# Interleaving the row blocks of a graph dilation, and pinning one load, in a two-layer graph network on one core

## The chip, the cores and the metric

The kernel runs on one core of a Trainium2 chip. A core has TensorE (PE, the matmuls; PEld is its weight loads), VectorE (DVE), ScalarE (ACT), GpSimd (POOL) and SyncE (SP), each with a queue of instructions that it takes in order. Sixteen DMA engines move data. Here SP issues the loads and POOL the stores. The metric is the device time of one execution in microseconds, as the median of several runs.

## The reference

There are 16 graphs (B) with 1024 nodes (N) and 128 features (D). `x` is B x N x D. `adj` is B x N x N with weights where there is an edge.

- **Layer 0**, three times per graph: `h @ W + b`, the cosine of all pairs of nodes, times `adj`, times `h`.
- **Dilation** of the graphs' patterns (`adj > 0`), which layer 1 needs. It is sequential in the rows: each row counts its neighbours, ranks them, removes those whose rank is a multiple of a step, and takes the same columns out of later rows:

```python
def step(carry, n):
    row = jnp.take(carry, n, axis=0)
    num = jnp.sum(row.astype(jnp.int32))
    sf = jnp.where(num > T_DIL, (num + K_DIL - 1) // K_DIL, 1)
    rank = jnp.cumsum(row.astype(jnp.int32))
    rm = row & (rank % sf == 0)          # and only where num > 1 and the mask is set
    carry = carry.at[n].set(row & ~rm)
    return carry.at[:, n].set(carry[:, n] & ~rm), None
```

- **Layer 1**, three graph convolutions ("sage" layers) on `adj * keep`, with a batch norm over all graphs behind each, then a projection and the residual `x2`, which is `x` after layer 0.

## The kernel before

**Two phases.** In the first, layer 0 and the dilation run side by side: layer 0 is mostly PE's work and dilation mostly DVE's and ACT's. In the second the three sage layers run, one after the other. In `residual` (L1055), within the last sage layer, each graph's `x2` is loaded back as `x2f` (L1058) and DVE adds it in (L1060, L1064). That tile has one buffer.

**Layer 0** (`layer0`, L439) is written as a generator that yields after each piece of work. Per graph and pass, `products` (L344) multiplies into a PSUM bank `pg`, of which there are two, and DVE multiplies the bank with `adj` into `ew` (L353 and L356), which empties it. `turn` (L373, L374) transposes `ew`, and `sums` (L384, L398) multiplies it with the features. Small tiles of PSUM share another two banks, `sm`: transposes, features, and dilation's `pdt`, `pT`, `pc` and `pe`.

**Dilation** (`dilation`, L545) goes through 16 blocks: 8 chunks `k` of 128 rows, each for two halves of 8 graphs. A block (`dilate`, L550) has three parts:

1. *Loads and tables* (L565 to L604). For each of 8 graphs, `an` (its rows of `adj`, L568) is loaded, and ACT makes the pattern of ones with Sign and Relu (L570, L571). For k > 0 what earlier chunks kept of these columns is loaded transposed as `kl` (L574), and DVE masks the pattern with it (L577). After every fourth graph, a table group: PE transposes the four diagonal blocks into `pdt` (L592), ACT copies them to `dT` (L594), PE makes `pT` (L599 to L601), and ACT writes the tables `T` (L603).
2. *Rounds* (L607 to L706). DVE finds zeros of T (`Z`, L615 or L618), then two to six rounds follow in which DVE compares (`E`, L650), PE counts (`pc`, L655 and L656), and DVE subtracts (L672). They end with a transpose of `E` (`pe`, L704, L705).
3. *Scans* (L709 to L744). For each graph DVE runs a cumulative sum over the 1024 columns (L722, `rank`, three buffers), ACT takes an absolute value (L731, Abs, one scan later in the text), DVE compares it into `kp` (L742), and POOL stores that as `keep` (L743).

The pattern has ten slots for eight graphs, so graphs 0 and 1 of the next block find a free slot, and graph i + 2 needs the slot that scan i of this block gives back. `an`, `kl`, `T` and `kp` have two buffers each.

**What sets the order.** `dilation` too yields a weight after each piece. The loop at L777 adds the weights up and runs layer 0's generator until it has come as far, in share of its own total, which it reaches at 0.93 of dilation's weight. This is the order of the program text. A planner then arranges each engine's queue: by its own estimates it may pull an instruction ahead of ones that stand before it in the text, if what it needs is there. `tc.keep_in_program_order` exempts an instruction from that; before, the Abs at L731 is the only one. In the hardware each queue is taken in order.

Of the kernel before, what the change touches and what calls it, by code (L numbers as in the profile page):

```python
# [16 lines left out]
P = 128  # L17
# [29 lines left out]
def tile_adj_preln_d2(  # L47
# [152 lines left out]
    with ExitStack() as actx:  # L200
# [344 lines left out]
        def dilation(exact=False):  # L545
            for k in range(NCH):
                for half in range(2):
                    yield from dilate(k, half, exact)

        def dilate(k, half, exact):  # L550
            nk = f"{'e' if exact else ''}{k}_{half}"
# [13 lines left out]
            for i in range(BH):  # L565
                b = half * BH + i
                an = poold.tile([P, N], F32, tag="an", name=f"an{nk}_{i}")
                nc.sync.dma_start(an, adj[b, cols, :])  # L568
                on = pattern(i)[:, 2 + k * P :]
                nc.scalar.activation(on, an[:, k * P :], AF.Sign)  # L570
                nc.scalar.activation(on, on, AF.Relu, accum_out=rest[:, i : i + 1])  # L571
                if k:
                    pk = poold.tile([P, NCH - 1, P], F16, tag="kl", name=f"kl{nk}_{i}")
                    nc.sync.dma_start(  # L574
                        pk[:, :k, :].rearrange("p j q -> p (j q)"), keep_d[b][: k * P, cols], transpose=True
                    )
                    nc.vector.scalar_tensor_tensor(  # L577
                        pattern(i)[:, 2 : 2 + k * P],
                        an[:, : k * P],
                        0.0,  # L580
                        pk[:, :k, :].rearrange("p j q -> p (j q)"),
                        ALU.is_gt,
                        ALU.mult,
                        accum_out=left[:, i : i + 1],
                    )
                yield 0.75
                if i % GT == GT - 1:
                    four = range(i - GT + 1, i + 1)
                    bs_ = slice(i - GT + 1, i + 1)
                    pdt = ps_sm.tile([P, GT, P], F16, tag="sm", name=f"pdt{nk}_{i}")  # L590
                    for n, ii in enumerate(four):
                        nc.tensor.transpose(pdt[:, n, :], pattern(ii)[:, diag], ident16)  # L592
                    dT = poold.tile([P, GT, P], F16, tag="dT", bufs=1, name=f"dT{nk}_{i}")
                    nc.scalar.activation(dT, pdt, AF.Copy)  # L594
                    nc.vector.tensor_scalar(rbias[:, bs_], rest[:, bs_], 2.0, -2.0, ALU.mult, ALU.add)
                    yield 0.1
                    pT = ps_sm.tile([P, GT, P], F32, tag="sm", name=f"pT{nk}_{i}")
                    for n, ii in enumerate(four):
                        nc.tensor.matmul(pT[:, n, :], lhsT=dT[:, n, :], rhs=upto, start=True, stop=False)  # L599
                        nc.tensor.matmul(pT[:, n, :], lhsT=pattern(ii)[:, diag], rhs=off, start=False, stop=False)  # L600
                        nc.tensor.matmul(pT[:, n, :], lhsT=ident16, rhs=after, start=False, stop=True)  # L601
                    for n, ii in enumerate(four):
                        nc.scalar.activation(T[:, ii, :], pT[:, n, :], AF.Identity, bias=rbias[:, ii : ii + 1])  # L603
                    yield 0.1  # L604


            x0 = poold.tile([P, BH], F32, tag="x0", name=f"x0{nk}")  # L607
            nc.vector.scalar_tensor_tensor(x0, left, -0.5, rest, ALU.add, ALU.add)
            nc.vector.tensor_tensor(x0, x0, mbias[:, half * BH : (half + 1) * BH, k], ALU.add)


            ends = exact or k >= LAST
            Z = poold.tile([P, BH, P], F16, tag="Z", name=f"Z{nk}")
            if ends:
                nc.vector.tensor_scalar(Z, T, 0.0, None, ALU.is_equal)  # L615
            else:
                found = poold.tile([P, 1], F32, tag="found", name=f"found{nk}")
                nc.vector.tensor_scalar(Z, T, 0.0, 0.0, ALU.is_equal, ALU.add, accum_out=found)  # L618
                nc.vector.tensor_tensor(astray[:, 0:1], astray[:, 0:1], found, ALU.add)
            E = poold.tile([P, BH, P], F16, tag="E", name=f"E{nk}")  # L620
            par = poold.tile([P, BH], F16, tag="par", name=f"par{nk}")

            def even(x, nm):

                ev = poold.tile([P, BH], F32, tag="ev", name=f"ev_{nm}")
                nc.vector.tensor_scalar(ev, x, EVENS, EVENS, ALU.add, ALU.subtract)
                return ev

            def removals(x, nm):


                if exact:
                    f, low = thresholds(x, nm)
                    at = poold.tile([P, 2, BH], F32, tag="at", name=f"at_{nm}")
                    nc.vector.scalar_tensor_tensor(at[:, 0, :], f, EVENS, low, ALU.subtract, ALU.max)
                    nc.vector.scalar_tensor_tensor(at[:, 0, :], x, 1.0, at[:, 0, :], ALU.is_le, ALU.add)
                    nc.vector.scalar_tensor_tensor(at[:, 1, :], f, EVENS, x, ALU.subtract, ALU.subtract)
                    nc.vector.tensor_tensor(par, at[:, 1, :], low, ALU.is_gt)
                    for i in range(BH):
                        nc.vector.tensor_scalar(  # L640
                            E[:, i, :], T[:, i, :], low[:, i : i + 1], at[:, 0, i : i + 1], ALU.max, ALU.is_equal
                        )
                else:
                    ev = even(x, nm)
                    mid = poold.tile([P, BH], F16, tag="mid", name=f"mid_{nm}")
                    nc.vector.scalar_tensor_tensor(mid, x, 1.0, ev, ALU.is_le, ALU.add)
                    if ends:
                        nc.vector.tensor_tensor(ev, ev, x, ALU.is_gt)
                        nc.vector.scalar_tensor_tensor(par, x, 1.0, ev, ALU.is_gt, ALU.mult)
                    nc.vector.tensor_tensor(E, T, mid.unsqueeze(2).to_broadcast([P, BH, P]), ALU.is_equal)  # L650
                pc = ps_sm.tile([P, BH], F32, tag="sm", name=f"pc_{nm}")
                for i in range(BH):
                    c = pc[:, i : i + 1]
                    if ends:
                        nc.tensor.matmul(c, lhsT=Z[:, i, :], rhs=par[:, i : i + 1], start=True, stop=False)  # L655
                    nc.tensor.matmul(c, lhsT=E[:, i, :], rhs=one16, start=not ends, stop=True)  # L656
                return pc

            if exact:
                x = poold.tile([P, BH], F32, tag="xe", bufs=1, name=f"xe_{nk}")  # L660
                nc.vector.tensor_copy(x, x0)
                with tc.For_i(0, P, 1):
                    pc = removals(x, f"e{nk}")
                    nc.vector.tensor_tensor(x, x0, pc, ALU.subtract)
            else:
                x = x0
                for r in range(ROUNDS[k]):
                    was = x
                    pc = removals(x, f"{nk}_{r}")
                    yield 1.0  # L670
                    x = poold.tile([P, BH], F32, tag="x", name=f"x_{nk}_{r}")
                    nc.vector.tensor_tensor(x, x0, pc, ALU.subtract)  # L672
                moved = poold.tile([P, BH], F32, tag="moved", name=f"moved_{nk}")
                nc.vector.tensor_tensor(moved, was, x, ALU.not_equal)
                nc.vector.tensor_tensor(astray, astray, moved, ALU.add)
            fin = poold.tile([P, 3, BH], F32, tag="fin", name=f"fin{nk}")
            radius, shift, none = fin[:, 0, :], fin[:, 1, :], fin[:, 2, :]
            if exact:

                f, low = thresholds(x, f"f{nk}")  # L680
                nc.vector.tensor_scalar(radius, x, 0.5, 0.5, ALU.add, ALU.mult)
                nc.vector.scalar_tensor_tensor(shift, f, EVENS, radius, ALU.subtract, ALU.subtract)
                nc.vector.tensor_tensor(radius, radius, low, ALU.max)
                nc.vector.scalar_tensor_tensor(shift, x, -2.0, shift, ALU.mult, ALU.add)
                nc.vector.scalar_tensor_tensor(radius, x, 1.0, radius, ALU.is_le, ALU.add)
            else:

# [473 lines left out]
```

## Time and profile before

| | us |
|---|---|
| median of 3 runs | 2893.7 (2886.03 to 2895.54) |
| the profiled execution | 2886.45 |
| its span, first to last instruction | 2884.7 |
| PE busy in it | 2661.2 (92%) |
| DVE busy | 1937.6 (67%) |
| ACT busy | 1427.3 (49%) |
| POOL busy | 468.7 (16%) |

PE's granted clock was 0.982 over the span. The first scan begins at 78 us and the last at 1563; layer 0's last matmul ends at about 1700, and the sage layers follow. A busy share that is an average over the span says little here, since the phases differ; so stretches and waits are read below.

In the profile, "A <- B" behind a wait means that A stood idle until B had released it. A row of a group has the line, engine, operation, output and inputs, shape and count, then the busy time in us with the mean of one in ns, then the idle time of the engine just before them with what ended it.

### The profile page before, as it was taken

What the parts mean: (1) busy time and instruction counts of PE and PEld (TensorE: products, weight loads), DVE (VectorE), ACT (ScalarE), POOL (GpSimd) and SP (SyncE); (2) the same over time, 40 slices, a digit from 0 to 9 for tenths busy, and PEclk for the clock granted to TensorE, in tenths of its full rate; (3) what the DMA queues carried; (4) which work ended last, traced back from release to release, by engine and by line L of the source; (5) the groups of instructions that cost most, each with busy time, mean ns of one, the idle gap of its engine ahead of it and who ended that gap; (6) DMA issues with size and microseconds to landing.
All of it is one profiled execution on the core that took longest, in us unless ns stands there. A gap on an engine that the chain in (4) does not pass through costs nothing. (4 is left out here: it accounts for less than half of the span.)

```text
span 2884.7 us, 52007 instructions
## 1 busy us (share of the span) xinstructions
PE 2661.2 (92%) x18803; PEld 2196.4 (76%) x18803; DVE 1937.6 (67%) x4913; ACT 1427.3 (49%) x4100; POOL 468.7 (16%) x619
## 2 busy tenths in 40 slices
PE   6899999899999999988998989999989999899997
PEld 4666676666666666666676779889879999899996
DVE  3788778877878788778877457777762333355554
ACT  6767667557556556455455333333333333333334
POOL 3111112011111111111112012222220010010101
PEclk9999999999999999999999999999999999999999
DMA  9447257347355475297063249999985666576764
GB/s 280 143 144 217 87 171 240 88 139 214 102 177 169 106 223 168 72 251 192 28 206 108 92 151 374 400 391 399 401 341 185 202 213 202 177 235 225 241 225 135
DMA packets 382234, 585.23 MB, mean 203 GB/s; under 512 B 85200, under 2 KB 266448, under 8 KB 381968
## 3 DMA queue, kind: packets, MB, share of 16 engines
q1 hardware_dynamic: 343280, 425.28, 47.1%
q0 software_dynamic: 38688, 156.53, 14.8%
q8 instruction: 151, 2.47, 0.4%
q14 instruction: 115, 0.94, 0.1%
HBM read 403.44 MB, written 163.58 MB: 197 GB/s over the span
## 5 line engine op out<-in xcount | busy, mean ns | idle before, releaser
L868 PE MATMUL agg<-hw,aT 128*128 128x128 f32 (+1 forms) x6144 | 742.9, 277 | 8.2 <-DVE aT L965 7.2
L868 PEld LDWEIGHTS agg<-hw,aT 128*128 128x128 f32 x6144 | 712.6, 192 | 13.3 <-DVE aT L965 9.7
L344 PE MATMUL pg<-nhT 128*128 128x512 f32 (+3 forms) x1152 | 457.2, 500 | 70.7 <-DVE ew L356 60.2
L384 PE MATMUL po<-ew,hS 128*128 128x512 f32 (+3 forms) x1152 | 457.4, 501 | 6.4 <-ACT hTo L407 3.6
L356 DVE TENSOR_TENSOR ew<-pg,adjA 128x768 f32<-128x768 f32 (+3 forms) x528 | 423.3, 824 | 0.5 <-PE pg L344 0.3
L398 PE MATMUL po<-ew,hS 128*128 128x128 f32 x2688 | 366.3, 276 | 0.0
L398 PEld LDWEIGHTS po<-ew,hS 128*128 128x128 f32 x2688 | 338.2, 192 | 35.4 <-issue 34.2
L374 ACT ACTIVATE ew<-gt 128x512 f32<-128x512 f32 (+1 forms) x480 | 209.0, 465 | 267.9 <-PE gt L373 260.6
L344 PEld LDWEIGHTS pg<-nhT 128*128 128x128 f32 x1152 | 189.3, 193 | 175.2 <-issue 130.4
L722 DVE TENSOR_TENSOR_SCAN rank<-patt 128x1024 f16<-128x1024 f16 x128 | 292.9, 2294 | 0.8
L384 PEld LDWEIGHTS po<-ew,hS 128*128 128x128 f32 x1152 | 196.4, 195 | 98.0 <-issue 67.3
L373 PEld LDWEIGHTS gt<-ident,ew 128*128 128x128 f32 x1344 | 169.8, 144 | 100.1 <-issue 74.8
L353 DVE TENSOR_TENSOR ew<-pg,adjA 128x128 f32<-128x128 f32 x384 | 107.2, 279 | 188.0 <-PE pg L344 142.8
L373 PE MATMUL gt<-ident,ew 128*128 128x128 f32 x1344 | 213.1, 278 | 4.3 <-PEq L802 2.4
L918 POOL TENSOR_TENSOR o<-o,rn 128x512 f32<-128x512 f32 x96 | 108.3, 1128 | 650.6 <-DVE rn L917 631.3
L840 PE MATMUL pw<-wrx,hT 128*128 128x256 f32 x768 | 180.5, 389 | 10.5 <-ACT hT L1032 9.7
L842 DVE TENSOR_TENSOR own<-pw,bs 128x256 f32<-128x256 f32 x192 | 81.3, 423 | 141.4 <-ACT hw L841 141.3
L840 PEld LDWEIGHTS pw<-wrx,hT 128*128 128x128 f32 x768 | 145.7, 195 | 32.9 <-ACT hT L1032 10.5
L913 ACT ACTIVATE own<-o 128x128 f32<-128x128 f32 x384 | 114.6, 301 | 111.1 <-DVE o L897 111.1
L897 DVE SCALAR_TENSOR_TENSOR o<-agg,invdeg,own 128x128 f32<-128x128 f32 x384 | 109.7, 344 | 86.9 <-PE agg L868 78.3
L983 ACT ACTIVATE aT<-pta 128x512 f32<-128x512 f32 (+3 forms) x160 | 71.2, 466 | 188.5 <-PE pta L982 180.7
L321 POOL TENSOR_TENSOR hS<-hN,rn 128x1024 f32<-128x1024 f32 x48 | 95.0, 1979 | 401.2 <-DVE rn L157 302.0
(165 smaller groups left out, 3940.4 us busy)
## 6 DMA issues: line engine op xcount, KB each, us to landing
an<-in_adj_dram SPq DMA_DIRECT2D x128, 512.0 KB, 4.7
keep<-kp POOLq DMA_DIRECT2D x128, 256.0 KB, 4.1
kb<-keep SPq DMA_DIRECT2D x128, 256.0 KB, 5.5
aT<-adT SPq DMA_DIRECT2D x32, 960.0 KB, 5.7
aT<-adT SPq DMA_DIRECT2D x32, 832.0 KB, 5.2
aT<-adT SPq DMA_DIRECT2D x32, 704.0 KB, 4.3
aT<-adT SPq DMA_DIRECT2D x32, 576.0 KB, 3.4
xb<-in_x_dram SPq DMA_DIRECT2D x31, 512.0 KB, 5.1
```

Of the source, the lines that this page charges most:

```text
L344: nc.tensor.matmul(pg[:, :n, :].rearrange("p c q -> p (c q)"), lhsT=self.nhT[:, q * P : (q + 1) * P], rhs=self.nhT[:, (q + c) * P : (q + c ...
L356: nc.vector.tensor_tensor(both[0][:, :, off, :], pg[:, own:n, :].unsqueeze(1).to_broadcast([P, 2, n - own, P]), both[1][:, :, off, :], ALU ...
L373: nc.tensor.transpose(pt[:, i, :], ew[:, at + i, :], ident)
L374: nc.scalar.activation(ew[:, at : at + n, :], pt[:, :n, :], AF.Copy)
L384: nc.tensor.matmul(self.po[:, c * P : (c + n) * P], lhsT=self.hS[:, q, :], rhs=ew[:, c - q : c - q + n, :].rearrange("p c q -> p (c q)"), ...
L398: nc.tensor.matmul(self.po[:, q * P : (q + 1) * P], lhsT=self.hS[:, q + n, :], rhs=ew[:, NCH - 1 - q + n, :], start=False, stop=closes and ...
L722: nc.vector.tensor_tensor_scan(rank, pt[:, 1 : N + 1], pt[:, 2:], 0.0, ALU.add, ALU.add)
L840: nc.tensor.matmul(pw[:, i, :], lhsT=hT[:, 2 * h + i, :], rhs=wrx[:, l, :], start=True, stop=True)
L868: nc.tensor.matmul(self.place(c), lhsT=aT[:, blk, :], rhs=self.hw[:, source, :], start=source == 0 and c % self.ga == 0, stop=ends(c, source),
L897: nc.vector.scalar_tensor_tensor(self.o[:, c, :], self.place(c)[:, :P], invdeg[:, b, c : c + 1], self.own[:, c, :], ALU.mult, ALU.add,)
L913: nc.scalar.activation(self.own[:, n, :], self.o[:, n, :], AF.Square, accum_out=ss[:, c : c + 1])
L918: nc.gpsimd.tensor_tensor(self.o[:, hc, :], self.o[:, hc, :], rn.unsqueeze(2).to_broadcast([P, CPH, D]), ALU.mult)
```

## The change

`dilate` no longer yields its work itself. It returns three generators, `loads`, `rounds` and `scans`, with the same instructions as before. `dilation` runs a block's rounds and then its scans, and after each of the eight scans takes one step of the next block's loads: one graph's pattern, and after the fourth and the eighth graph a table group. The first block's loads run ahead of its rounds as before, and the last block's scans have none beside them. A step of the loads yields 0.8 in place of 0.75 for each graph and 0.1 twice for each group. The exact variant, which runs only if a check on the data finds something (`n_off > 0`), keeps its order.

In `residual` the `x2f` load is exempt from the planner.

Cut to its core (the bodies of the three generators are the text above, indented):

```diff
         def dilation(exact=False):
-            for k in range(NCH):
-                for half in range(2):
-                    yield from dilate(k, half, exact)
+            blocks = [(k, half) for k in range(NCH) for half in range(2)]
+            loads = ()
+            for n, block in enumerate(blocks):
+                if not loads:
+                    loads, rounds, scans = dilate(*block, exact)
+                yield from loads
+                yield from rounds
+                this, loads = scans, ()
+                if n + 1 < len(blocks) and not exact:
+                    loads, rounds, scans = dilate(*blocks[n + 1], exact)
+                for scanned, weight in this:
+                    yield weight
+                    if scanned and loads:
+                        yield next(loads)
...
-            for i in range(BH):
+            E = radius = shift = low = None
+
+            def loads():
+                for i in range(BH):
...
-                yield 0.75
-                if i % GT == GT - 1:
...
-                    yield 0.1
...
-                    yield 0.1
+                    yield 0.8
+
+            def rounds():
+                nonlocal E, radius, shift, low
...
+            def scans():
...
-                    yield 2.5
+                        yield True, 2.5
...
-                yield 0.8
+                    yield False, 0.8
+
+            return loads(), rounds(), scans()
...
         def residual(b):
             x2 = pool2.tile([P, NCH, D], F32, tag="x2", bufs=1, name=f"x2f_{b}")
-            nc.sync.dma_start(x2, x2_d[b].rearrange("(c p) d -> p c d", p=P))
+            tc.keep_in_program_order(nc.sync.dma_start(x2, x2_d[b].rearrange("(c p) d -> p c d", p=P)))
```

## The prediction, made before the changed kernel ran

> **What bounds the kernel now.** I read the busy time of each engine in stretches first, then PE's waits, then the dilation's rows, then one piece of the timeline. The first answer cuts the run at 1580 us, where the last scan ends, and around 1700, where layer 0 ends. Its columns are the stretch, its length, and each engine's busy time with its number of instructions.
>
> ```profile
> 60.00:1580.00 1520.00, 1394.25 (x8745) 1012.80 (x8744) 1206.71 (x2842) 914.42 (x2431) 245.90 (x318) 0.98 0.53 156
> 1580.00:1700.00 120.00, 117.02 (x661) 84.65 (x660) 53.86 (x134) 37.64 (x114) 8.75 (x6) 1.00 0.19 65
> 1700.00:1740.00 40.00, 30.95 (x240) 28.97 (x238) 25.10 (x77) 15.36 (x44) 7.35 (x13) 0.91 0.88 316
> ```
>
> PE (first busy column) is what bounds it: busy for 1394 of 1520 us while dilation and layer 0 run together, and its work isn't touched. All that this part can give back is PE's idle time, 125.7 us. PE's waits there, longest first (total, times, longest):
>
> ```profile
> PE pg L344 <- DVE ew L356: 60.1, 41, 5.2
> PE pc L656 <- DVE E L650: 10.9, 13, 1.5
> PE pg L344 <- DVE rn L157: 7.2, 4, 2.8
> ```
>
> Half of it is one wait: layer 0's product needs one of two `pg` banks, and VectorE (DVE) hasn't emptied them. No later row is over 5.3 us. So I ask when DVE is late. The next two answers take blocks 2 to 15 (of 16): first the stretches from a block's first scan to its last `kp`, then what lies between them, where the next block's tables and rounds are made. These are the sums over the 14 stretches of each.
>
> ```profile
> sum 855.00, PE 761.54 PEld 546.60 DVE 738.86 ACT 547.60 POOL 160.52; mean PE 54.40 PEld 39.04 DVE 52.78 ACT 39.11 POOL 11.47
> ...
> sum 499.00, PE 480.73 PEld 357.46 DVE 344.53 ACT 251.15 POOL 60.86; mean PE 34.34 PEld 25.53 DVE 24.61 ACT 17.94 POOL 4.35
> ```
>
> Among scans DVE is 86.4% busy (738.86/855) and PE idles 93.5 us, 10.9%. Between them DVE is 69.0% busy and PE idles 18.3 us, 3.7%. That unevenness is what the change can level. The rows of the dilation itself:
>
> ```profile
> L722 DVE TENSOR_TENSOR_SCAN rank<-patt 128x1024 f16<-128x1024 f16 x128 | 292.9, 2294 | 0.8
> L731 ACT ACTIVATE rank<-rank,fin 128x1024 f16<-128x1024 f16 x128 | 145.9, 1146 | 0.4 <-DVE rank L722 0.4
> L742 DVE TENSOR_SCALAR kp<-rank,fin 128x1024 f16<-128x1024 f16 x128 | 74.3, 581 | 55.3 <-ACT rank L731 52.9 <-DMA keep<-kp 1.7
> L570 ACT ACTIVATE patt<-an 128x896 f16<-128x896 f32 (+7 forms) x121 | 79.5, 662 | 128.0 <-DMA an<-in_adj_dram 68.0 <-DVE rank L722 59.4 <-DVE kp L742 0.6
> ```
>
> **The change, part by part.** *Nothing is added or removed.* The same 128 scans, 112 masks (L577), 32 table groups and 128 `kp` are issued, with the same DMAs: per block 8 `an`, 8 `kl` (but for k = 0) and 8 `keep`. The weights that pace layer 0 agree too (8 x 0.8 = 8 x 0.75 + 4 x 0.1), so dilation ends beside the same layer-0 work; in the two instruction orders PE has equal layer-0 columns behind the last `pe`, within 1%. The tail of 120 us stays.
>
> *What moves.* I compared the orders of the built programs. The loads hardly move: in both, 91 of 112 masks stand between the scans of the block before, since the planner had already pulled each load up to the scan that frees its slot. SP's queue has the same runs of `an` and `kl`, and POOL's queue the same `keep` stores. So I price DMA and both queues at nothing; their cover is that the transfers had been early already. What moves is the spacing of scans and the tables. Counted in layer 0's `ew` instructions, a clock that PE sets, blocks 2 to 14 have 319 of 681 between their first and last scan before, and 389 after. With the rows' durations DVE then has 1.90 us of work for each `ew` among scans and 1.56 elsewhere before; 1.72 and 1.72 after. The level is even.
>
> *What evening is worth.* The two stretches give two points, idle 3.7% at 69% and 10.9% at 86.4%. On a straight line evening gains nothing: at the common 80% (1083.4/1354) PE idles the same 112 us. On a curve that grows as load/(1 - load), which fits both points (2.23 x 1.7 = 3.7; 6.35 x 1.7 = 10.8), 80% gives 6.8%, 92 us: a gain of 20 us, 21 with the first blocks. Ends: 0 and -21. Against the upper end, the small scale gets worse: neighbouring scans with at most one `ew` between them go from 20 to 30 of 127. I take two thirds, **-14**. This is my choice, not a row.
>
> *A rule against it.* The Trainium skill ("Perfetto Trace Analysis", Optimizing Scalar/DVE Operations) says that where Scalar or Vector isn't saturated but makes bubbles on another engine, breaking up instructions may help. A scan stays one piece of 2.29 us. By that rule alone the evening is worth 0; by the stretches -14. The wait row has 41 waits of 1.5 us on average and a longest of 5.2, over two scans long, so queues of several instructions matter besides the single scan; I keep the row's reading.
>
> *Tables among the scans: a wait added.* A table group on ACT is `dT` (0.59 us) and four `T` (0.37 each), 2.06 us, and waits for PE's `pdt` and `pT`, 25.1 + 25.0 us over 31 groups, 1.6 each. Before, no scan's Abs (L731) stands close behind a group; after, 15 of 32 groups have one directly behind, 26 within two layer-0 instructions. The skill ("PSUM — Partial Sum Buffer", Engine vs sequencer instructions) calls these queues strict FIFO; the `kp` row agrees, as its 52.9 us are waits for an Abs. Behind a late Abs stands `kp` on DVE, and behind that `ew`, whom PE waits for. At most 26 x 3.7 = 96 us of DVE stall. Below, it may be 0 or a gain, since `kp` now also stands further back and the Abs has more time. By the nearest row, 37 waits of 1.4 us, 26 more are 37 us of DVE time, in an engine that is idle a fifth of the time. I put a tenth on PE, 3.7: **+4**, with ends -10 and +48 (half of the 96).
>
> *x2's load.* The planner had pulled the last layer's first `x2f` load to the start of phase two:
>
> ```profile
> 1713.88 0.37 SPq L1058 DMA_DIRECT2D x2f<-x  x1
> ...
> 1725.20 0.87 DVE L1060 SCALAR_TENSOR_TENSOR x2f<-blb,mf,x2f 128x128 f32<-128x128 f32 x3 [7.87 <-DMA x2f<-x]
> ...
> 1727.81 0.50 PEld L982 LDWEIGHTS pta<-ident,aT 128*128 128x128 f32 x3 [6.83 <-issue]
> 1727.84 0.88 PE L982 MATMUL pta<-ident,aT 128*128 128x128 f32 x3 [6.69 <-issue]
> ```
>
> It lands after 11 us, DVE waits 7.87 us for it with the masks of row 4 behind, and PE stands still for 6.69 us. Pinned, the load goes to the last layer and the stall goes. Next late is the mask chain (L959, L965, L969, 1.6 us), whose rows were issued at 1708, so I take **-6**, ends -6.7 and 0. In that layer every `x2f` load now stands behind its batch's third `aT` row rather than ahead of the batch's first; behind it on SP wait five rows, and on DVE L897. PE is 60.00 of 60 us busy there, with a sums bank to spare, and a load of 5 us: 0, at worst +10.
>
> **Sum.** -14 + 4 - 6 = -16. Against the profiled execution's own time, 2886.45 (span 2884.7), that is 2870.5; the median of the runs shown, 2893.7, is 7.25 above that execution, and so I predict 2877.7, rounded to **2878 us**. A measurement of this kernel can tell about 0.3%, 8.7 us, from no change.
>
> **Rivals.**
> (a) *It doesn't do what it says:* the loads were early already, and the straight line holds. Only x2 remains: -6, 2888. For it: 91 of 112 both times, and more scan pairs. Against: 1.72 and 1.72.
> (b) *Slower:* ACT's queue takes the place of the evened load. At the Abs behind the table groups, 96 us of stall, half of which reaches PE: +48; with -14 and -6, and in place of the +4, it is +28, 2922. It makes the kernel slower than before once `kp`'s waits for the Abs, 52.9 us, grow by 40 (half of 40 uses up the 20). For it: 26 groups against none. Against: the planner set `kp` back as well, and T's 16 us of waits at `Z` (L615, L618) may shrink.
> (c) *Better than the curve:* the waits for `ew` halve (-30), and `kp` and `kl` waits fall with them (-10), and x2's -6: 2848.
>
> **How the numbers follow.** Forecast 47% (own range 2862 to 2890), (a) 20%, (b) 27%, (c) 6%. The range for 8 in 10 goes from 2850, close to (c), to 2910, which takes in the lower half of (b). Faster by over 0.3% (below 2885) are most of the forecast, a little of (a), and (c): 0.51. Within it are the rest of the forecast, most of (a) and the edge of (b): 0.22. Slower is (b) with a piece of (a): 0.27.
>
> **What will show it.** Right: PE's wait `pg` for `ew` falls from 60 to 45 us or less, the idle shares among and between the scans come close to each other, and the 6.69 us gap at `pta` is gone. Wrong: `kp`'s waits for the Abs grow beyond 80 us with PE's `pg` wait above 60 (b), or both shares stay put though the scans are spread (a). A PE gap in the last layer would make the zero for x2's new place wrong.

## The result, and the profile after

| | before | after |
|---|---|---|
| median of 20 runs, us | 2888.55 (2881.39 to 2895.54) | 2877.09 (2871.27 to 2890.45) |
| the profiled execution | 2886.45 | 2874.98 |
| its span | 2884.7 | 2873.2 |

The ratio is 0.9965, with a 95% interval of 0.9955 to 0.9975. So the kernel is faster by 0.35% (10 us) by the ratio, and by 11.5 us by the medians. The median of before, 2893.7 from three runs, came down to 2888.55 with twenty.

Where the 11.5 us came from is read by cutting both traces at the same events (us; in brackets the time in it in which PE stood idle; worked out from the instructions of the two traces; layer 0 is taken to end with its last multiplication with the features, `po`):

| stretch | before | after |
|---|---|---|
| start to first scan | 78.1 (25.6) | 77.0 (24.2) |
| first to last scan | 1487.6 (123.2) | 1478.4 (117.1) |
| to layer 0's last `po` matmul | 134.0 (3.0) | 133.7 (2.9) |
| to the second sage layer's first matmul of aggregation (`agg`, the 2049th) | 468.8 (41.0) | 469.3 (39.4) |
| the rest | 716.2 (30.8) | 714.8 (30.4) |

Nearly all of it is between the first scan and the last: 9.2 us, 6.1 of which are idle time of PE. The other 3.1 are a shorter busy time of PE, which isn't traced further. The lines of after stand 17 to 20 further down: the scan is L740, Abs L749, `kp` L760, `E` L667. The same stretches as before:

```profile
60.00:1570.00 1510.00, 1389.78 (x8737) 1013.20 (x8736) 1205.15 (x2858) 911.44 (x2428) 249.05 (x319) 0.98 0.53 157
1570.00:1689.00 119.00, 116.11 (x654) 84.36 (x653) 53.77 (x134) 37.10 (x113) 8.44 (x6) 1.00 0.19 66
1689.00:1729.00 40.00, 37.33 (x323) 35.01 (x321) 31.23 (x84) 18.22 (x53) 8.01 (x15) 1.00 0.89 321
1729.00:1769.00 40.00, 33.22 (x275) 31.79 (x275) 24.94 (x59) 12.20 (x41) 10.19 (x15) 0.91 1.03 376
```

The tail kept its length (119 us from last scan to cut, 120 before). In the first 40 us of phase two PE is 37.33 us busy where it was 30.95: the gap at `x2f` is gone. In the next 40 it is 33.22. The DMA share stands at 1.03 there (the last but one column). The timeline of after shows what happened:

```profile
1737.63 0.69 DVE L989 SCALAR_TENSOR_TENSOR aT<-aT,both 128x512 f32<-128x512 f32 x1 [6.51 <-DMA aT<-in_adj_dram]
...
1738.43 1.09 PE L1002 MATMUL pta<-ident,aT 128*128 128x128 f32 x4 [5.98 <-DVE aT L989]
```

The same `pta` waits 5.98 us again, 11 us later and for a row of the second graph: the wait moved. The DMA engines are full in this stage (1.03), which fits; the runs of part 1 show that it moves, not that this is why.

PE's waits up to layer 0's end (total, times, longest):

```profile
PE pg L344 <- DVE ew L356: 65.5, 52, 3.8
...
PE pc L673 <- DVE E L667: 4.0, 9, 0.8
...
PE pg L344 <- DVE rn L157: 1.0, 1, 1.0
```

The wait that the forecast was about, `pg` for `ew`, did **not** fall: 65.5 us after 60.1. The small one in the rounds, `pc` for `E`, fell from 10.9 to 4.0, and a small one of layer 0, `pg` for `rn`, from 7.2 to 1.0. Then the sums over the 14 stretches from a block's first scan to its last `kp`, and over the 14 between them:

```profile
sum 1098.00, PE 999.40 PEld 724.41 DVE 867.29 ACT 685.01 POOL 189.70; mean PE 71.39 PEld 51.74 DVE 61.95 ACT 48.93 POOL 13.55
...
sum 230.00, PE 222.66 PEld 167.25 DVE 201.42 ACT 103.09 POOL 30.85; mean PE 15.90 PEld 11.95 DVE 14.39 ACT 7.36 POOL 2.20
```

Among scans PE idles 98.6 us of 1098, 9.0%, with DVE 79.0% busy. Between them, where only rounds are left, it idles 7.3 of 230, **3.2%**, with DVE 87.6% busy. The more loaded stretch is the one that costs less. So one rising curve over DVE's load can't be right. The dilation's rows:

```profile
L740 DVE TENSOR_TENSOR_SCAN rank<-patt 128x1024 f16<-128x1024 f16 x128 | 295.0, 2316 | 0.9
L749 ACT ACTIVATE rank<-rank,fin 128x1024 f16<-128x1024 f16 x128 | 146.7, 1151 | 30.8 <-DVE rank L740 30.2 <-DVE fin L712 0.5
L760 DVE TENSOR_SCALAR kp<-rank,fin 128x1024 f16<-128x1024 f16 x128 | 68.6, 547 | 49.9 <-ACT rank L749 49.4
```

The counts are the same and the busy times nearly so, and `kp` waits for the Abs 49.4 us, where it waited 52.9: rival (b) isn't seen.

### The profile page after: what moved, and what is told of

Its sections match the earlier page's. It is cut to its first block, busy times and chain, and to the rows that moved or that the text cites. A ratio compares the mean times of both kernels' runs of the same rounds, so it can differ in the third digit from the quotient of the medians.

```text
span 2873.2 us, 51953 instructions
## 1 busy us (share of the span) xinstructions
PE 2659.3 (93%) x18803; PEld 2199.0 (77%) x18803; DVE 1939.7 (68%) x4913; ACT 1426.0 (50%) x4100; POOL 473.7 (16%) x619
## 5 line engine op out<-in xcount | busy, mean ns | idle before, releaser
L344 PE MATMUL pg<-nhT 128*128 128x512 f32 (+3 forms) x1152 | 460.2, 502 | 69.5 <-DVE ew L356 65.5
L740 DVE TENSOR_TENSOR_SCAN rank<-patt 128x1024 f16<-128x1024 f16 x128 | 295.0, 2316 | 0.9
L860 PE MATMUL pw<-wrx,hT 128*128 128x256 f32 x768 | 179.5, 388 | 10.5 <-ACT hT L1052 9.7
L860 PEld LDWEIGHTS pw<-wrx,hT 128*128 128x128 f32 x768 | 145.0, 194 | 32.6 <-ACT hT L1052 10.5
L749 ACT ACTIVATE rank<-rank,fin 128x1024 f16<-128x1024 f16 x128 | 146.7, 1151 | 30.8 <-DVE rank L740 30.2
```

The lines of the kernel that those rows point to most:

```text
L344: nc.tensor.matmul(pg[:, :n, :].rearrange("p c q -> p (c q)"), lhsT=self.nhT[:, q * P : (q + 1) * P], rhs=self.nhT[:, (q + c) * P : (q + c ...
L740: nc.vector.tensor_tensor_scan(rank, pt[:, 1 : N + 1], pt[:, 2:], 0.0, ALU.add, ALU.add)
L749: nc.scalar.activation(rank, rank, AF.Abs, bias=shift[:, i : i + 1], scale=1.0 if exact else -1.0)
L860: nc.tensor.matmul(pw[:, i, :], lhsT=hT[:, 2 * h + i, :], rhs=wrx[:, l, :], start=True, stop=True)
```

## The experiments

Each ratio is to the kernel before, timed on the same chip. The medians come from three chips, on which before took 2887.13 us (parts 1 and 2, and after with pinned scans), 2883.39 (before with pinned scans, and part 4) and 2888.35 (parts 5 to 7), so kernels of different parts are compared by their ratios. The letters in the expectations: in part 1, A says that the pin of `x2f` is worth nothing, and B that it is worth 6 us. From part 2 on, A says that the mean density of DVE's work sets what PE loses; C, that an Abs behind a table group costs; D, that the gain comes from tables being ready early; E, that PE's `pg` waits are made by scans that the planner puts close together; G, that the length of one scan makes them.

**1. The pin by itself, both ways.** The first kernel is after without it, the second is before with it.

```diff
-            tc.keep_in_program_order(nc.sync.dma_start(x2, x2_d[b].rearrange("(c p) d -> p c d", p=P)))
+            nc.sync.dma_start(x2, x2_d[b].rearrange("(c p) d -> p c d", p=P))
```

> The changed kernel with x2's load not exempt from the planner, so that the first x2f load stands at the start of phase two again. Theory A (all of the gain is dilation's; phase two is bound by its DMA there, so the 6.7 us gap that went at row 4 of the first graph came back as a 6.0 us gap in the second): as the changed kernel, 2877 within 4 us, and the stretch from the first to the 2048th agg matmul stays at 459 to 460 us. Theory B (the pin is worth the 6 us that were forecast): 2883.

> The kernel before, with the pin alone. Theory A (the pin is worth nothing): 2888 within 4 us, a ratio of 0.999 to 1.001. Theory B (it is worth 6 us): 2882, a ratio of 0.998. Either way dilation's part of the span, up to layer 0's last matmul at 1700 us, is as before within 3 us.

Without it 2880.06 us, 0.9979 of before (0.9964 to 0.9993). With it alone 2888.08, 0.9997 (0.9986 to 1.0009), so the forecast 6 us (0.2%) lie outside the interval, which leaves at most 4. Without it the median is 3 us above after's, and the two intervals overlap, so that run alone decides nothing. The timeline of before with the pin has a gap at the same place as after:

```profile
1745.52 0.83 PE L982 MATMUL pta<-ident,aT 128*128 128x128 f32 x4 [4.87 <-DVE aT L969]
```

After without the pin has the gap where before has it (6.42 us, at 1717.5 us) and none over 2 us at the second graph. From the first `agg` to the second sage layer's first it takes 458.1 us with the pin alone, 459.3 before, 459.8 after and 459.1 in after without it. The pin is worth nothing that shows here.

**2. The masks among the scans, the tables behind them.** After, but each table group (PE's `pdt` and `pT`, ACT's `dT` and `T`) waits until the block's last scan, as in before:

```diff
+                    yield 0.75
+                for i in range(BH):
                     if i % GT == GT - 1:
...
-                    yield 0.8
+                        yield 0.2
```

> The changed kernel, but only the patterns of the next block are made among the scans; both of its table groups (pdt, dT, pT, T) stand behind the last scan, as before the change. Theory A (the gain is the lower density of VectorE work among scans, and a table group has hardly any VectorE work): within 4 us of 2877. Theory C (an Abs behind a table group in ScalarE's queue costs some us, which the changed kernel pays): faster than it, 2870. Theory D (the gain is that tables are ready sooner, so that rounds start without a gap): back to 2886.

2898.75 us, 1.0044 of before (1.0029 to 1.006): slower than both. Its waits, of PE and then of DVE:

```profile
PE pg L344 <- DVE ew L356: 59.6, 46, 3.3
PE pc L675 <- DVE E L669: 11.2, 13, 2.2
```

```profile
DVE Z L637 <- ACT T L620: 24.3, 8, 4.8
```

The same wait of `Z` in before, then in after:

```profile
DVE Z L618 <- ACT T L603: 11.7, 5, 4.2
```

```profile
DVE Z L635 <- ACT T L618: 14.8, 7, 3.7
```

`pc` waits 11.2 us again, as before: where the tables are made moves this wait, some 7 us. D's own reason isn't seen. `Z` waits for the tables longer after the change than before (14.8 against 11.7), and in all three traces it starts only 0.1 to 0.2 us behind the last table on average. What goes with `pc` is how much of layer 0 stands beside the rounds: between `Z` and the first scan of blocks 2 to 16 DVE has 106 `ew` in before, 155 in after and 107 here.

`pc` is the smaller part of what this order loses. It is 0.8% (23 us) slower than after, more than A, C or D expected. Between first and last scan PE idles 139.9 us, where it idles 117.1 in after, and `pg` isn't higher. The rest is spread over small waits of layer 0, such as `pt_a` for its load (11.1 after 7.3), `pt_h` for `x` (9.2 after 6.2) and `po` for `hTo` (8.2 after 5.4). Why they grow stays open.

**3. The spacing of scans by itself.** In after, 30 of 127 neighbouring scans have at most one `ew` between them on DVE, in before 20. The text doesn't put them so: the planner pulls scans forward. Exempt from the planner, each scan stays where the text has it:

```diff
-                        nc.vector.tensor_tensor_scan(rank, pt[:, 1 : N + 1], pt[:, 2:], 0.0, ALU.add, ALU.add)
+                        tc.keep_in_program_order(
+                            nc.vector.tensor_tensor_scan(rank, pt[:, 1 : N + 1], pt[:, 2:], 0.0, ALU.add, ALU.add)
+                        )
```

The same edit was made in after and in before:

> The changed kernel with every scan exempt from the planner, so that it stays where the text puts it: neighbouring scans with at most one ew between them fall from 30 of 127 to 10, while VectorE's work and its mean density among the scans stay. Theory A (mean density alone sets TensorE's idle time): 2877 within 4 us and a wait of pg for ew of 60 to 65 us. Theory E (runs of scans set it): the wait falls below 50 us, and the time to 2865.

> The kernel before, with every scan exempt from the planner (and nothing else): neighbouring scans with at most one ew between them fall from 20 of 127 to 3. Theory E (what TensorE loses among scans is set by runs of scans on VectorE): the wait of pg for ew falls from 60 us to below 40, and the time by 30 us or more, to 2857 or less. Theory A (mean density sets it): the density among scans stays, 2888 within 5 us. If E holds, its distance to the changed kernel with pinned scans (2827) is what the interleaving is worth when scans do not run in pairs: under 10 us if spacing was all, some 30 us if the level of the density counts as well.

In after it gives 2826.9 us, 0.979 of before (0.9773 to 0.9806): 50 us faster than after, far more than expected. In before it gives 2844.42, 0.9863 (0.9839 to 0.9886). PE's waits, first of after so pinned, then of before so pinned:

```profile
PE pg L344 <- DVE ew L356: 37.5, 36, 3.2
...
PE pc L673 <- DVE E L667: 3.6, 8, 0.8
```

```profile
PE pg L344 <- DVE ew L356: 40.1, 42, 3.7
...
PE pc L656 <- DVE E L650: 10.6, 13, 1.5
```

This tells two effects apart. `pg` falls to some 40 us in both, interleaved or not, once the close pairs of scans are gone (10 and 3). `pc` falls only where the tables are made early. That is E for the large wait, and the place of the tables for the small one. With pinned scans, too, the interleaved kernel is faster, by 0.7% (21 us; 0.9863 against 0.979; the intervals don't meet), but see 5 for the scatter. That lies between the "under 10" of spacing alone and the "some 30" of a level that counts as well. In the traces PE idles 13.0 us less for it between first and last scan (94.6 and 81.6), more than the 7 of `pc`.

**4. Which instruction makes the wait?** Three variants of after with pinned scans: masks pinned as well (as the scan above, at L594); masks and `kp` pinned; the Abs freed:

```diff
-                    tc.keep_in_program_order(
-                        nc.scalar.activation(
-                            rank, rank, AF.Abs, bias=shift[:, i : i + 1], scale=1.0 if exact else -1.0
-                        )
+                    nc.scalar.activation(
+                        rank, rank, AF.Abs, bias=shift[:, i : i + 1], scale=1.0 if exact else -1.0
```

> The changed kernel with scans pinned and the masks of the next block (L594) pinned too: masks that stand directly beside a scan fall from 33 of 112 to 7, stretches of over 6 us of VectorE work between two ew from 38 to 32. Theory E: some 5 to 10 us below 2827, with the wait of pg for ew below 37 us. Theory A: 2827 within 4 us. Risk: a pinned mask waits for its load at its place, and VectorE's waits for kl grow.

> As the one with scans and masks pinned, and kp pinned as well: one pair of neighbouring scans, 27 stretches of over 6 us of VectorE work between two ew. Theory E: a little faster again, 2815 to 2822. Against it: with three kinds of instruction fixed, waits of VectorE for Abs and loads at fixed places (55 us for Abs with scans pinned) grow, and the time rises above 2830.

> The changed kernel with scans pinned, but the Abs no longer: the planner then moves it ahead of the table groups on ScalarE, so that an Abs stands within two instructions behind a group 1 time in place of 25. It also sets scans closer against ew: 27 neighbours in place of 10. Theory C (the Abs behind a table group costs): VectorE's waits of kp for Abs fall from 55 us to under 30. If that wait is what TensorE pays for, the time falls below 2820; if pairs of scans weigh more (theory E), it rises to 2850 or so although the waits of kp fall.

| pinned | us | ratio to before | close scans | `pg` for `ew` | `kp` for Abs |
|---|---|---|---|---|---|
| Abs (before) | 2888.55 | 1 | 20 | 60.1 | 52.9 |
| Abs (after) | 2877.09 | 0.9965 (0.9955 to 0.9975) | 30 | 65.5 | 49.4 |
| Abs, scans | 2826.9 | 0.979 (0.9773 to 0.9806) | 10 | 37.5 | 55.5 |
| Abs, scans, masks | 2845.21 | 0.9869 (0.9846 to 0.9891) | 7 | 26.5 | 60.3 |
| Abs, scans, masks, `kp` | 2835.04 | 0.9832 (0.9812 to 0.9852) | 1 | 18.4 | 58.0 |
| scans | 2857.13 | 0.9908 (0.9884 to 0.9933) | 27 | 58.6 | 14.6 |

Read the last three columns together. The kernels with 20 close scans or more have 58.6 to 65.5 us of `pg`, those with 10 or fewer 18.4 to 37.5 (before with pinned scans, above: 3 and 40.1). It is two groups rather than a slope: the late tables of part 2 have 31 close scans and 59.6 us, so going from 20 to 30 isn't shown to cost anything. The runs vary what is pinned; that the closeness of scans makes the wait, and not something else in the new orders, is read from these counts. `kp`'s wait for the Abs doesn't go with it at all. With the Abs free it falls to 14.6 us, and yet `pg` is back at 58.6, with 27 close scans again, as E expected. The expectations for pinned masks, alone and with `kp`, missed: `pg` fell, but the time rose, with masks alone by 0.8% (0.9869 against 0.979). PE idles 96.9 us there between first and last scan, where it idles 81.6 with pinned scans only. Other waits had grown, such as the one for features, 11.4 us in that kernel after 4.1, and in the kernel with all pinned:

```profile
PE pg L344 <- DVE ew L356: 18.4, 27, 3.2
...
PE po L384 <- ACT hTo L407: 13.3, 13, 2.1
```

**5. Is it luck of the planner's order?** Two kernels with weights shifted a little (`yield 0.8` to 1.0 for a load, 2.5 to 2.3 for a scan), the first on after, the second on after with pinned scans:

```diff
-                    yield 0.8
+                    yield 1.0
...
-                        yield True, 2.5
+                        yield True, 2.3
```

> The changed kernel with the weights of a load and a scan at 1.0 and 2.3 in place of 0.8 and 2.5, the same sum: nothing is pinned, added or moved to another part of the text, only the spacing shifts a little and the planner's choices with it. This measures how far an equal kernel scatters. If the 10 us of the change are the interleaving's: within 5 us of 2877. If they are within the planner's luck: more than 8 us off, to either side.

> The same weights with scans pinned. As above: within 5 us of 2827 if an order of this kind has a time of its own, 8 us or more off if the scatter of equal orders is as large as the steps between the kernels with pinned scans (2827, 2835, 2845).

On after: 2876.46 us, 0.9955 (0.9939 to 0.997), with `pg` at 60.7 and `pc` at 3.0. So the change's 10 us hold under another order. On pinned scans: 2838.15, 0.9818 (0.9793 to 0.9842). By the medians that is 11 us above the kernel it was made from, by the ratios 8 (the intervals overlap), and in the two traces layer 0 ends 8.4 us later. So two equivalent orders with pinned scans can lie some 10 us apart. In part 4 the kernel with all pinned lies 12 us above the one with scans and Abs pinned, by the ratios, which such a scatter could make; with masks and scans it is 23 us, more than twice that, but with two orders measured it isn't read as an effect of its own.

**6. Smaller pieces.** The scan in two pinned halves of 512 columns, the second starting from the last column of the first:

```diff
-                        nc.vector.tensor_tensor_scan(rank, pt[:, 1 : N + 1], pt[:, 2:], 0.0, ALU.add, ALU.add)
...
-                        yield True, 2.5
+                        H = N // 2
+                        tc.keep_in_program_order(
+                            nc.vector.tensor_tensor_scan(rank[:, :H], pt[:, 1 : H + 1], pt[:, 2 : H + 2], 0.0, ALU.add, ALU.add)
+                        )
+                        yield False, 1.25
+                        tc.keep_in_program_order(
+                            nc.vector.tensor_tensor_scan(
+                                rank[:, H:], pt[:, H + 1 : N + 1], pt[:, H + 2 :], rank[:, H - 1 : H], ALU.add, ALU.add
+                            )
+                        )
+                        yield True, 1.25
```

> The changed kernel with scans pinned, each scan cut into two halves of 512 columns (the second begins with the first's last value), both pinned, with 1.25 of weight between them. VectorE has 128 more instructions and some 15 us more work. Theory G (the grain: one instruction of 2.29 us outlasts what the two pg banks cover): the wait of pg for ew falls from 37 to below 25 us, and the time by 10 us or more, below 2817. Theory E without grain (only runs of several long instructions cost): 2827 to 2840, the added work being paid.

2819.76 us, 0.9763 (0.974 to 0.9786). The rows of the halves, then PE's wait:

```profile
L748 DVE TENSOR_TENSOR_SCAN rank<-patt,rank 128x512 f16<-128x512 f16 x128 | 168.0, 1313 | 0.6
L742 DVE TENSOR_TENSOR_SCAN rank<-patt 128x512 f16<-128x512 f16 x128 | 155.4, 1217 | 0.1
```

```profile
PE pg L344 <- DVE ew L356: 26.6, 39, 2.0
```

DVE works 28 us more (168.0 + 155.4 = 323.4 against 295.0), and PE waits less for it: 26.6 us, longest 2.0, against 37.5 and 3.2. The wait went the way that the size of a piece would have it (G), though not below the 25 us that were expected. The time, 8 us lower by the ratios (0.9763 against 0.979), can't be told from the scatter.

**7. The best version.** In the kernels up to part 5 some 130 us of layer 0 are left behind the last scan. The loop over dilation (L799 of after) lets layer 0 come to SPREAD of its *own* total by dilation's end, and the rest follows alone; the description ahead of the prediction, "at 0.93 of dilation's weight", had this the wrong way round. As pinned scans leave PE less idle, more of layer 0 is put beside them:

```diff
-SPREAD = 0.93
+SPREAD = 0.97
```

> The changed kernel with scans pinned and SPREAD at 0.97 in place of 0.93, so that dilation ends later beside layer 0: its last scan stands behind 864 of the 912 ew in place of 826. The 132 us of layer 0 behind the last scan, where TensorE loses only 3 us, shrink to some 75, and the same VectorE work is spread over 4% more. By the density among scans (0.85 to 0.82) a gain of 3 to 8 us, 2819 to 2824; none, or a loss, if the first loads of phase two, which wait for dilation's end, come late (a gap of TensorE at the first agg).

**2811.47 us, 0.9732 of before (0.9708 to 0.9756)**: 77 us faster than before, 66 faster than the change. The stretch behind the last scan went from 132.5 to 77.5 us, and layer 0 ends at 1624.5 us (1646.8 without the new share). The step from pinned scans to this, 0.6% or 17 us, is more than the 3 to 8 us expected and less than twice the scatter of part 5; it was measured in one order only. The stretch from 60 us to there, with the columns as above:

```profile
60.00:1624.50 1564.50, 1486.57 (x9402) 1086.98 (x9401) 1260.99 (x2992) 948.28 (x2543) 259.30 (x323) 1.00 0.53 157
```

PE is busy 95.0% (1486.57/1564.5), and the granted clock is 1.00 against 0.98. Halves and the new share together were not tried.

## Why the prediction was right, and where not

**The time** was right: 2878 forecast, 2877.09 measured. Much of that is luck: -16 us was forecast and -11.5 measured, from a base that was 5 us too high, and of the terms -14, +4 and -6 the first was too large and the other two came to nothing. None of the three signs of being right came. `pg` rose to 65.5 us in place of 45 or less; the idle shares went from 10.9% and 3.7% to 9.0% and 3.2%, no closer; and the gap at `pta` moved.

**No work added, DMA and queues at nothing, the same tail:** right. The tail is 133.7 us after 134.0, and the rows of the dilation have the same counts. The largest of PE's waits for a load, `pt_a`, is 7.3 us after the change and 5.3 before.

**Evening, -14:** the time up to layer 0's end fell by 10.6 us (1699.7 to 1689.1), so the size is near, but the mechanism is wrong. The step that failed is the curve load/(1 - load), drawn through two points. With its factor of 1.7 it gives 12.0% idle for after's rounds (87.6% of DVE; 7.06 x 1.7) and 6.4% for its scans (79.0%; 3.76 x 1.7); 3.2% and 9.0% were measured. Over both, PE idles 8.0% after (105.9 of 1328 us) and 8.3% before (111.8 of 1354): 5.9 us less, nearly the straight line. The scan stretches differ from the others in what DVE's work is made of (2.3 us pieces, several in a row), not only in how much there is. Before with pinned scans shows it directly: between a block's first scan and last `kp` DVE is 90.0% busy there, more than the 86.4% without the pin, and PE idles 8.1% (66.0 of 820.2 us) instead of 10.9%. Of the two kernels with pinned scans the less loaded one still idles less: after so pinned has DVE 82.7% busy and PE 6.1% idle. The prediction had named the order of DVE's queue ("neighbouring scans ... from 20 to 30", "queues of several instructions matter") but priced it as a third off the curve.

What went down instead are two small waits that the sum didn't have: `pc` for `E` by 6.9 us and `pg` for `rn` by 6.2, against 5.4 more of `pg` for `ew`. Only the fall of `pc` is there in every order. All four kernels that make tables behind the scans (before, before with the `x2f` load pinned, before with scans pinned, after with late tables) have `pc` at 10.5 to 11.2 us; in all ten that make them among the scans it is between 3.0 and 5.6. The other two don't hold: with shifted weights `rn` is 4.2 and `pg` 60.7. From `Z` to the first scan a block takes 19.7 us on average in after, 16.8 in before, as more of layer 0's work stands beside it. That PE waits less in the rounds because of this work is argued; no run moved the one without the other.

**Tables among the scans, +4:** no wait was added (`kp` for Abs 52.9 to 49.4), and rival (b), 27%, fell with it. It counted Abs instructions behind a group and not how far `kp` stands behind the Abs. The kernel with a free Abs shows more: `kp`'s wait fell to 14.6 without `pg` being lower than in before. Close scans came back in that kernel, so a small cost isn't excluded. What stood against the rival, that the 16 us of waits for T at `Z` may shrink, didn't come: the two rows of after have 14.8 and 6.7 us.

**x2's load, -6:** wrong, nothing of it shows. The term took the gap for the price. "Next late is the mask chain ... whose rows were issued at 1708" looked at one graph; the next graph's rows came late, with the DMA share at 1.03, and the 6 us came up there. Zero for the load's new place was right: in the last third of `agg` PE idles 0.6 us in both.

**The rule against it.** The Trainium skill ("Perfetto Trace Analysis", Optimizing Scalar/DVE Operations) on breaking up instructions, weighed at 0 against -14, was nearer to the mechanism than the reading by load: evening the load left the `pg` waits, and halves of a pinned scan cut them by 11 us, with a gain in time that the scatter covers.

**Rival (a)**, only x2 remains, was right that the straight line nearly holds (8.3% and 8.0%), and wrong on where the gain is: x2 gave nothing, and the interleaved dilation some 10 us.

## What to carry to other kernels

A busy share of the feeding engine doesn't say what the bound engine loses. List what stands *in a row* on the feeding engine at the waits, and look whether a planner put it there; pinning the longest instruction in its place gave 50 us here, more than the rewriting of the order, and pinning more instructions gave no more. Before a gap in a stage is booked as a gain, ask whether that stage's DMA is full: here the gap moved and didn't go. And two kernels that differ only in order differed by some 10 us, so an effect of that size needs a second order.

## What was not expected of the hardware

Idle time of PE that gathers costs a second time. These are two neighbouring stretches of 3.4 us of after, twice (granted clock in the third column from the end):

```profile
159.00:162.40 3.40, 0.82 (x8) 0.63 (x6) 3.40 (x4) 3.21 (x7) 0.00 (x0) 0.98 0.00 0
162.40:165.80 3.40, 2.97 (x5) 1.79 (x6) 3.23 (x10) 1.34 (x9) 0.00 (x0) 0.52 0.00 0
384.40:387.80 3.40, 0.75 (x8) 0.59 (x6) 3.40 (x7) 2.63 (x6) 1.89 (x1) 0.96 0.58 176
387.80:391.20 3.40, 3.40 (x11) 2.26 (x12) 1.74 (x7) 0.00 (x0) 0.00 (x0) 0.53 0.81 235
```

PE is busy 0.82 and 0.75 of 3.4 us, and in the next 3.4 us the clock is at half. In the records the half clock comes in pieces of 3.41 us or twice that. All 12 such pieces of before between 60 us and layer 0's end, and all 14 of after, follow 3.4 us in which PE idled 1.9 to 3.3 us; it need not have been idle throughout. Cut into the same slots of 3.41 us, these two traces have in that stretch no slot with 1.83 us of idle time or less that is followed by a half clock, and none with 1.89 or more that isn't. A product `pg` takes 847 ns in such a piece and 592 elsewhere (medians).

If half of PE's busy time in these pieces counts as lost, that is an estimate of 27.1 us up to layer 0's end in before, 26.4 after, 17.6 with pinned scans and 6.2 in the best version. So of the 44.3 us that pinned scans took from after's stretch between first and last scan, 35.5 were idle time and 8.8 a shorter busy time, which is about the size of the clock's part. The prediction's "all that this part can give back is PE's idle time" was too narrow by that much.
